# A bilinear interaction kernel: x turned by half as many transposes with straight and crosswise copies, and w cut at the edges of steps

## The chip, the cores and the metric

The kernel runs on one core of a Trainium2 chip. The metric is the device time of one execution in microseconds (us). Before the change it is 1345.8 us, the median of three runs (1344.6 to 1345.83). The profiled execution spans 1343.8 us.

## The reference

The input x holds 4096 samples (B) of 32 fields (F), each a vector of 64 numbers (D), in float32. For each of the 496 pairs of fields i < j there is a 64x64 matrix W. The output is, for every sample and pair, the vector x_i times W, multiplied elementwise by x_j:

```python
idx_i, idx_j = np.triu_indices(F, k=1)      # 496 pairs, ordered by i, then j
vi = inputs[:, idx_i, :]
vj = inputs[:, idx_j, :]
vidots = jnp.einsum('bpd,pde->bpe', vi, W)
return vidots * vj                          # 4096 x 496 x 64 float32
```

The output has 520 MB, x has 33.6 MB and W 8.1 MB. The profile counts 41.68 MB read from HBM and 520.09 MB written.

## The kernel before

The batch is taken in 16 blocks of 256 samples, each as NB = 2 tiles of 128 samples, so there are 32 tiles. `p0[i]` is the number of the first pair with left field i.

**Loads of w.** The 496 matrices are loaded as rows of 4096 numbers (16 KB), one pair to an SBUF partition, in four parts. Parts 0, 1 and 2 go out on SyncE's queue, between the loads of x, part 3 later on ScalarE's queue:

```python
cuts = [*range(0, NP, P), NP]               # 0, 128, 256, 384, 496
wrows = list(zip(cuts[:-1], cuts[1:]))
...
def load_w(c, eng=nc.sync):
    a, b = wrows[c]
    raw[c] = pool.tile([P, D * D], F32, tag=tag, name=f"raw_{c}")
    eng.dma_start(out=raw[c][: b - a, :], in_=wflat[a:b])
...
new_x(0)
load_x(0, nc.sync, 0, 1)                    # the first tile of block 0
load_w(0)
load_w(1)
load_x(0, nc.sync, 1, NB)
load_w(2)
new_x(1)
load_x(1, nc.sync)
```

Each part is then reordered (`order_w`, copies on VectorE, GpSimd or ScalarE), turned by TensorE (`turn_w`) and copied into `wT[c]`, where columns 0 to 31 of every W lie on partitions 0 to 63, one row of W to a partition, and columns 32 to 63 on partitions 64 to 127. Part 0 is done ahead of everything; the reorder copies and turns of parts 1 to 3 stand between the first steps:

```python
for c, orders, turns in (
    (1, (2, 4, 8, 10), (4, 7, 12, 15)),     # at these places of the schedule
    (2, (17, 22, 27, 32), (19, 24, 29, 34)),
    (3, (54, 54, 55, 55), (57, 60, 63, 66)),
):
```

**Turning x.** The matmul needs each field with D on the partitions. As the two halves of W's columns lie on different halves of the partitions, each field is needed on both halves. A transpose turns two neighbouring fields at once, and the kernel before takes overlapping pairs (s, s+1), (s+1, s+2), ..., so each field is turned twice: once into the lower, once into the upper half. A slot of zeros stands ahead of field 0.

```python
RUN = 2 * BANK // P                          # 8
def turn_x(blk, k, q, copy):
    pt = psum.tile([P, RUN, P], F32, tag="ps", name=...)
    for n in range(RUN):
        s = k * F + q * RUN + n
        nc.tensor.transpose(pt[:, n, :], xs[blk][:, s : s + 2, :].rearrange("p f d -> p (f d)"), ident)   # line 143
    xT = xtpool.tile([P, RUN, P], F32, tag="xT", name=...)
    copy(xT, pt)                             # line 147, on ScalarE
    return xT
...
AHEAD = 4                                    # a group is asked for so many steps early
at = place[t, first[q * RUN - 1] if q else 0] - AHEAD
```

**Steps.** A step takes up to CH = 16 pairs with the same left field. Two matmuls, one for each half of W's columns, fill two PSUM banks; a step that straddles two parts of w takes two for each part. VectorE multiplies by x_j into an output tile, or, for some steps (`aside`), ScalarE copies and GpSimd multiplies:

```python
for c, (lo, hi) in enumerate(wrows):
    lo, hi = max(pa, lo), min(pa + m, hi)
    if lo < hi:
        for h in range(2):
            n = i + 1 - h
            nc.tensor.matmul(                # line 244
                ps[:, h, lo - pa : hi - pa, :],
                xT[blk, kt, n // RUN][h * D : (h + 1) * D, n % RUN, :],
                wT[c][h * D : (h + 1) * D, lo - wrows[c][0] : hi - wrows[c][0], :],
                start=True, stop=True)
...
if i in aside and c0 == 0 and s not in no_aside:
    nc.scalar.copy(tmp, src)                 # line 258
    nc.gpsimd.tensor_mul(dst, tmp, xj)       # line 259
else:
    nc.vector.tensor_mul(dst, src, xj)       # line 261
```

**Outputs.** The pairs of a tile are cut into five groups of about 100 pairs. Each has an output tile (`ot`, three buffers, of which parts 0 and 1 of w use two at the start), and when its last step is done SyncE sends it to HBM in one transfer. The first three tiles are interleaved group by group, so that the later parts of w are needed later.

**Loads of x** after the first two blocks go out on ScalarE's queue in one transfer of 128 rows. For every third block the load is cut: 120 rows on GpSimd's queue in two transfers, and the other 8 rows in two transfers of 5 and 3 rows on ScalarE's queue (`load_fifteen`). `turn_engines` sends small transfers on GpSimd's queue.

Of the kernel before, what the change touches and what calls it, by code (L numbers as in the profile page):

```python
# [8 lines left out]
F32 = mybir.dt.float32  # L9
# [3 lines left out]
def kernel(  # L13
# [16 lines left out]
    nc = tc.nc  # L30

    B, F, D = x.shape
    P = 128
    NB = 2
    assert 2 * D == P and B % (NB * P) == 0
    NBLK = B // (NB * P)
    NP = F * (F - 1) // 2
    E2 = D // 2
    BANK = 512
    CH = BANK // E2  # L40
    RUN = 2 * BANK // P
    p0 = [i * (F - 1) - i * (i - 1) // 2 for i in range(F)]


# [3 lines left out]

    aside = (1, 3, 5, 7, 9, 11, 13)

    cuts = [*range(0, NP, P), NP]
    wrows = list(zip(cuts[:-1], cuts[1:]))

    const = ctx.enter_context(tc.tile_pool(name="const", bufs=1))
    xpool = ctx.enter_context(tc.tile_pool(name="xpool", bufs=2))
    xtpool = ctx.enter_context(tc.tile_pool(name="xtpool", bufs=4))
    tpool = ctx.enter_context(tc.tile_pool(name="tpool", bufs=4))
    opool = ctx.enter_context(tc.tile_pool(name="opool", bufs=3))
    psum = ctx.enter_context(tc.tile_pool(name="psum", bufs=4, space=bass.MemoryType.PSUM))

    ident = const.tile([P, P], F32, tag="ident", name="ident")
    make_identity(nc, ident)

    xs = {}

    def rows_of(dram: bass.AP, blk: int) -> bass.AP:
        return dram[blk * NB * P : (blk + 1) * NB * P]

    def new_x(blk: int):

        xs[blk] = xpool.tile([P, 1 + NB * F, D], F32, tag="xs", name=f"xs_{blk}")
        nc.gpsimd.memset(xs[blk][:, 0, :], 0.0)  # L72

    def load_x(blk: int, eng, k0: int = 0, k1: int = NB):
        src = rows_of(x, blk).rearrange("(p k) f d -> p (k f) d", k=NB)
        eng.dma_start(out=xs[blk][:, 1 + k0 * F : 1 + k1 * F, :], in_=src[:, k0 * F : k1 * F, :])

# [6 lines left out]
    def turn_engines(k: int):  # L86
        n = k if k > 1 else 17
        c = used[0] % 8
        used[0] += 1
        src = x[: NB * n].rearrange("(p k) f d -> p k f d", k=NB)  # L90
        tc.keep_in_program_order(
            nc.gpsimd.dma_start(out=scratch[:n, :, c : c + 1], in_=src[:, :, 0, 0:1])  # L92
        )

    def load_fifteen(blk: int):
        rows = rows_of(x, blk).rearrange("(p k) f d -> p k f d", k=NB)
        dst = xs[blk][:, 1:, :].rearrange("p (k f) d -> p k f d", k=NB)
        for a, b in ((SWR, SWR + 5), (SWR + 5, P)):
            nc.scalar.dma_start(out=xs[blk][a:b, 1:, :], in_=rows[a:b].rearrange("p k f d -> p (k f) d"))
        for h in range(2):  # L100
            cut = slice(h * F // 2, (h + 1) * F // 2)
            tc.keep_in_program_order(
                nc.gpsimd.dma_start(out=dst[:SWR, :, cut, :], in_=rows[:SWR, :, cut, :])  # L103
            )
            turn_engines(1)
# [7 lines left out]
    def load_w(c: int, eng=nc.sync):  # L113

        a, b = wrows[c]
        pool, tag = ((opool, "ot"), (opool, "ot"), (const, "w3"), (const, "w3"))[c]
        raw[c] = pool.tile([P, D * D], F32, tag=tag, name=f"raw_{c}")
        eng.dma_start(out=raw[c][: b - a, :], in_=wflat[a:b])

    def order_w(c: int, k: int, copy):  # L120
        r = wrows[c][1] - wrows[c][0]
        rp = tpool.tile([P, EU, 2, D], F32, tag="tmp", name=f"rp_{c}_{k}")
        src = raw[c][:r, :].rearrange("p (d h e) -> p e h d", h=2, d=D)
        copy(rp[:r], src[:, k * EU : (k + 1) * EU])  # L124
        return rp

    def turn_w(c: int, k: int, rp, copy):
        r = wrows[c][1] - wrows[c][0]
        if c not in wT:
            wT[c] = const.tile([P, r, E2], F32, tag=f"w{c}", name=f"wT_{c}")  # L130
        pt = psum.tile([P, EU, P], F32, tag="ps", name=f"ptw_{c}_{k}")
        for n in range(EU):
            nc.tensor.transpose(  # L133
                pt[:, n, :r], rp[:r, n].rearrange("p h d -> p (h d)"), ident[:r, :r]
            )
        copy(wT[c][:, :, k * EU : (k + 1) * EU], pt[:, :, :r].rearrange("p e r -> p r e"))  # L136

    def turn_x(blk: int, k: int, q: int, copy):

        pt = psum.tile([P, RUN, P], F32, tag="ps", name=f"ptx_{blk}_{k}_{q}")  # L140
        for n in range(RUN):
            s = k * F + q * RUN + n
            nc.tensor.transpose(  # L143
                pt[:, n, :], xs[blk][:, s : s + 2, :].rearrange("p f d -> p (f d)"), ident
            )
        xT = xtpool.tile([P, RUN, P], F32, tag="xT", name=f"xT_{blk}_{k}_{q}")
        copy(xT, pt)  # L147
        return xT


# [8 lines left out]
    first = {}  # L159
# [11 lines left out]
    place = {ts: n for n, ts in enumerate(sched)}  # L171


    AHEAD = 4
    due: dict = {}
    for t in range(NT):
        for q in range(F // RUN):
            at = place[t, first[q * RUN - 1] if q else 0] - AHEAD
            due.setdefault(max(0, at), []).append(("x", t // NB, t % NB, q))
    for c, orders, turns in (  # L180
        (1, (2, 4, 8, 10), (4, 7, 12, 15)),
# [9 lines left out]
    loads[place[LEAD, LATE]] = 2  # L191

    new_x(0)
    load_x(0, nc.sync, 0, 1)
# [6 lines that stand above are left out]
    turn_engines(5)  # L201

    v, p, a = nc.vector.tensor_copy, nc.gpsimd.tensor_copy, nc.scalar.copy
    xT, rps = {}, {}
    xT[0, 0, 0] = turn_x(0, 0, 0, a)
    due[0] = [d for d in due[0] if d != ("x", 0, 0, 0)]
    for k, copy in enumerate((v, v, v, a)):
# [5 lines left out]
    for s, (t, st) in enumerate(sched):  # L213
        blk, kt = divmod(t, NB)
        g, i, c0, m = steps[st]
        if s in loads:
            new_x(loads[s])
            if loads[s] % 3 == 1:
                load_fifteen(loads[s])
            else:  # L220
                load_x(loads[s], nc.scalar)
        for what, *args in due.get(s, ()):
            if what == "x":
                xT[tuple(args)] = turn_x(*args, a)
            elif what == "turn":
                turn_w(*args, rps.pop(tuple(args)), a)
            else:
                c, k = args
                rps[c, k] = order_w(c, k, (v, v, p, v)[c] if k % 2 == 0 else (v, v, p, a)[c])
                if (c, k) == (2, NU - 1):  # L230
                    load_w(3, nc.scalar)

        base, end = groups[g]
        pa = p0[i] + c0
        if pa == base:
            ots[t] = opool.tile([P, cap, D], F32, tag="ot", name=f"ot_{t}_{g}")
        ot = ots[t]
        ps = psum.tile([P, 2, CH, E2], F32, tag="ps", name=f"ps_{s}")
        for c, (lo, hi) in enumerate(wrows):
            lo, hi = max(pa, lo), min(pa + m, hi)  # L240
            if lo < hi:
                for h in range(2):
                    n = i + 1 - h
                    nc.tensor.matmul(  # L244
                        ps[:, h, lo - pa : hi - pa, :],
                        xT[blk, kt, n // RUN][h * D : (h + 1) * D, n % RUN, :],
                        wT[c][h * D : (h + 1) * D, lo - wrows[c][0] : hi - wrows[c][0], :],
                        start=True,
                        stop=True,
                    )  # L250
        o = pa - base
        j = 1 + kt * F + i + 1 + c0
        dst = ot[:, o : o + m, :].rearrange("p m (h e) -> p m h e", h=2)
        src = ps[:, :, :m, :].rearrange("p h m e -> p m h e")
        xj = xs[blk][:, j : j + m, :].rearrange("p m (h e) -> p m h e", h=2)
        if i in aside and c0 == 0 and s not in no_aside:
            tmp = tpool.tile([P, CH, 2, E2], F32, tag="tmp", name=f"tmp_{s}")
            nc.scalar.copy(tmp, src)  # L258
            nc.gpsimd.tensor_mul(dst, tmp, xj)  # L259
        else:  # L260
            nc.vector.tensor_mul(dst, src, xj)  # L261

        ends = (p0[2], end) if s < NS and (t, g) == (0, 0) else (end,)
        if pa + m in ends:
            n0 = p0[2] if len(ends) > 1 and pa + m == end else base
            nc.sync.dma_start(
                out=rows_of(out, blk).rearrange("(p k) n d -> p k n d", k=NB)[:, kt, n0 : pa + m, :],
                in_=ot[:, n0 - base : pa + m - base, :],
            )
# [28 lines left out]
```

## Time and profile before

| | before |
|---|---|
| time, median of 3 | 1345.8 us |
| span of the profiled execution | 1343.8 us |
| mean granted TensorE clock | 0.959 |
| transposes of x on PE (line 143) | 1024, 142.0 us busy |
| matmuls on PE (line 244) | 6272 records, 1017.8 us busy |
| copies of turned x on ScalarE (line 147) | 128 of 1012 ns, 129.5 us |
| multiplications on VectorE (line 261) | 1252, 944.8 us |
| output transfers | 161, 2880 to 3360 KB most of them, 16.3 to 17.1 us from issue to landing |
| mean DMA rate | 419 GB/s |

The span is the time from the first to the last instruction on the core. An engine's busy share is an average over the whole span. TensorE is shown as PE (matmuls and transposes) and PEld (loads of the stationary operand), VectorE as DVE, ScalarE as ACT, GpSimd as POOL and SyncE as SP. The row DMA gives the mean busy share of the core's 16 DMA engines, and GB/s what they moved. In a list of waits each line names who waited for whom, the sum in us, the number of times and the longest. In a line of the timeline, brackets hold the idle time ahead of it and what ended it; `x3` is a count of instructions merged into the line.

### The profile page before, as it was taken

The page shows a single profiled execution, that of the slowest core. Times are in us where ns is not written, and L with a number is a line of the kernel's source. Part 1 is how long each engine was busy: PE and PEld are TensorE (multiplying, and loading weights), DVE is VectorE, ACT ScalarE, POOL GpSimd, SP SyncE. Part 2 cuts the span into 40 slices and gives each one's busy share as a digit, 9 for nine tenths or more (in the row PEclk, how much of TensorE's full clock was granted, in tenths as well). Part 3 has the DMA queues.
Part 4 walks back from the last instruction along what each step waited for, and adds up shares of the span by engine and source line. Part 5 has one row for each costly group of instructions (what it writes and reads, how often), then busy time and mean ns, then how long its engine had stood idle before and what let it go on. Part 6 is the DMA issues. An engine that isn't in the chain of part 4 may idle for free.

```text
span 1343.8 us, 17902 instructions
## 1 busy us (share of the span) xinstructions
PE 1163.9 (87%) x7424; PEld 680.1 (51%) x7424; DVE 956.0 (71%) x1262; ACT 374.1 (28%) x367; POOL 544.7 (41%) x264
## 2 busy tenths in 40 slices
PE   6989889888898888888889888888988889989894
PEld 4555545545455454455445554444554545545552
DVE  5778767766677677776758777576876767767774
ACT  3432222223232232222232222232222323223321
POOL 1813424444243445333444434442444424344431
PEclk9989999999999899998989999899899989989997
DMA  9999999999999999999999999999999999999997
GB/s 394 371 427 410 427 422 433 429 421 430 422 430 426 431 427 407 427 424 429 432 420 424 404 424 431 425 430 416 419 421 411 428 425 427 423 423 431 423 415 320
DMA packets 28258, 562.95 MB, mean 419 GB/s; under 512 B 3456, under 2 KB 3456, under 8 KB 5504
## 3 DMA queue, kind: packets, MB, share of 16 engines
q1 hardware_dynamic: 24048, 530.59, 93.0%
q10 hardware_dynamic: 1632, 23.33, 4.2%
q0 software_dynamic: 2496, 7.88, 1.5%
q8 instruction: 58, 0.95, 0.3%
q14 instruction: 24, 0.20, 0.0%
HBM read 41.68 MB, written 520.09 MB: 418 GB/s over the span
## 4 chain that ended last, share of the span: by engine, by line
DMA 50%; PE 23%; DVE 16%; POOL 6%; issue 3%; ACT 1%; DVEq 0%; SPq 0%; POOLq 0%; ACTq 0%
DMA out_dram<-ot 50%; PE ps L244 18%; DVE ot L261 16%; POOL ot L259 5%; PE ptx L143 4%; PE ptw L133 1%; DMA raw<-in_L_rec_W_dram 1%; POOL scratch L92 1%; ACT tmp L258 1%; POOL xs L103 0%; DVE rp L124 0%; POOL rp L124 0%; DVEq L261 0%; ACT wT L136 0%; POOL xs L72 0%
## 5 line engine op out<-in xcount | busy, mean ns | idle before, releaser
L261 DVE TENSOR_TENSOR ot<-ps,xs 128x1024 f32<-128x1024 f32 (+15 forms) x1252 | 944.8, 810 | 356.8 <-DMA out_dram<-ot 193.8
L244 PE MATMUL ps<-wT,xT 64*128 64x512 f32 (+13 forms) x6272 | 1017.8, 467 | 122.4 <-DVE ot L261 110.7
L244 PEld LDWEIGHTS ps<-wT,xT 64*128 64x128 f32 x6272 | 552.7, 193 | 553.1 <-DVE ot L261 289.0
L259 POOL TENSOR_TENSOR ot<-tmp,xs 128x1024 f32<-128x1024 f32 x220 | 519.0, 2360 | 622.1 <-ACT tmp L258 438.7
L258 ACT COPY tmp<-ps 128x1024 f32<-128x1024 f32 x220 | 222.7, 1012 | 468.3 <-PE ps L244 401.2
L147 ACT COPY xT<-ptx 128x1024 f32<-128x1024 f32 x128 | 129.5, 1012 | 451.1 <-PE ptx L143 451.1
L143 PE MATMUL ptx<-ident,xs 128*128 128x128 f32 x1024 | 142.0, 283 | 35.9 <-DVE ot L261 27.5
L143 PEld LDWEIGHTS ptx<-ident,xs 128*128 128x128 f32 x1024 | 111.8, 143 | 82.5 <-issue 41.9
L72 POOL MEMSET xs<- 128x64 f32 x16 | 2.4, 151 | 148.5 <-DVE ot L261 148.5
L133 PE MATMUL ptw<-ident,rp 128*128 128x128 f32 (+1 forms) x128 | 18.6, 298 | 3.9 <-DVE rp L124 3.9
L133 PEld LDWEIGHTS ptw<-ident,rp 128*128 128x128 f32 (+1 forms) x128 | 15.6, 156 | 10.3 <-DVE rp L124 5.0
L136 ACT COPY wT<-ptw 128x1024 f32<-128x1024 f32 (+1 forms) x15 | 14.8, 984 | 20.9 <-PE ptw L133 20.9
L124 DVE COPY rp<-raw 128x1024 f32<-128x1024 f32 (+1 forms) x9 | 10.7, 1221 | 10.8 <-DMA raw<-in_L_rec_W_dram 10.8
L92 POOL DMA_DIRECT2D scratch<-in_r_inputs_dram x10 | 9.1, 908 | 0.2 <-issue 0.2
L124 POOL COPY rp<-raw 128x1024 f32<-128x1024 f32 x4 | 7.9, 1979 | 0.1
L124 ACT COPY rp<-raw 112x1024 f32<-112x1024 f32 (+1 forms) x3 | 5.9, 1958 | 5.0 <-POOL ot L259 3.2
L103 POOL DMA_DIRECT2D xs<-in_r_inputs_dram x8 | 6.0, 753 | 1.4 <-issue 1.4
L136 DVE COPY wT<-ptw 128x1024 f32<-128x1024 f32 x1 | 1.2, 1224 | 2.9 <-PE ptw L133 2.9
L147 ACT ACT_TABLE_LOAD x1 | 1.3, 1283 | 0.7 <-PEq L285 0.7
masks.py:197 POOL MEMSET ident<- 128x128 f32 x1 | 0.2, 204 | 0.3 <-POOLq L285 0.3
masks.py:199 POOL TENSOR_SCALAR_AFFINE_SELECT ident<-ident 128x128 f32<-128x128 f32 x1 | 0.3, 288 | 0.0
L285 POOL MEMSET const-float32-0.0<- 128x1 f32 x1 | 0.1, 93 | 0.3 <-issue 0.3
(3 smaller groups left out, 0.3 us busy)
## 6 DMA issues: line engine op xcount, KB each, us to landing
out_dram<-ot SPq DMA_DIRECT2D x64, 3360.0 KB, 16.3
out_dram<-ot SPq DMA_DIRECT2D x32, 3168.0 KB, 16.4
out_dram<-ot SPq DMA_DIRECT2D x32, 3104.0 KB, 17.0
out_dram<-ot SPq DMA_DIRECT2D x31, 2880.0 KB, 17.1
xs<-in_r_inputs_dram ACTq DMA_DIRECT2D x10, 2048.0 KB, 17.3
xs<-in_r_inputs_dram POOLq DMA_DIRECT2D x8, 960.0 KB, 31.5
raw<-in_L_rec_W_dram SPq DMA_DIRECT2D x3, 2048.0 KB, 17.1
xs<-in_r_inputs_dram SPq DMA_DIRECT2D x2, 1024.0 KB, 5.2
```

The costliest lines, as they stand in the source:

```text
L72: nc.gpsimd.memset(xs[blk][:, 0, :], 0.0)
L92: nc.gpsimd.dma_start(out=scratch[:n, :, c : c + 1], in_=src[:, :, 0, 0:1])
L103: nc.gpsimd.dma_start(out=dst[:SWR, :, cut, :], in_=rows[:SWR, :, cut, :])
L124: copy(rp[:r], src[:, k * EU : (k + 1) * EU])
L133: nc.tensor.transpose(pt[:, n, :r], rp[:r, n].rearrange("p h d -> p (h d)"), ident[:r, :r])
L136: copy(wT[c][:, :, k * EU : (k + 1) * EU], pt[:, :, :r].rearrange("p e r -> p r e"))
L143: nc.tensor.transpose(pt[:, n, :], xs[blk][:, s : s + 2, :].rearrange("p f d -> p (f d)"), ident)
L147: copy(xT, pt)
L244: nc.tensor.matmul(ps[:, h, lo - pa : hi - pa, :], xT[blk, kt, n // RUN][h * D : (h + 1) * D, n % RUN, :], wT[c][h * D : (h + 1) * D, lo - ...
L258: nc.scalar.copy(tmp, src)
L259: nc.gpsimd.tensor_mul(dst, tmp, xj)
L261: nc.vector.tensor_mul(dst, src, xj)
```

## The change

The change has two parts.

**x.** Each field is turned once, in pairs that don't overlap: four transposes for eight fields, 16 for a tile of 32 fields in place of 32. Three ScalarE copies then write the result twice: straight (`xT[:, 0]`), and crosswise (`xT[:, 1]`), the lower half of the partitions to the upper half and the upper to the lower, so that every field is again on both halves. The slot of zeros goes, with its memset. A group of turned fields is asked for six steps ahead of the first step that uses it.

**w.** The parts end at pairs 118 = p0[4], 243 = p0[9], 371 = p0[15] + 11 and 496, so that two of the three inner cuts fall on edges of steps. The parts have 118, 125, 128 and 125 rows in place of 128, 128, 128 and 112. How a part is loaded (`load_w`) stays as it is.

The purpose is to take work from TensorE: fewer transposes, and fewer steps that need two matmuls a half.

```diff
--- before.py
+++ after.py
@@ -38,7 +38,7 @@
     E2 = D // 2
     BANK = 512
     CH = BANK // E2
-    RUN = 2 * BANK // P
+    RUN = 8
     p0 = [i * (F - 1) - i * (i - 1) // 2 for i in range(F)]
 
 
@@ -48,7 +48,7 @@
 
     aside = (1, 3, 5, 7, 9, 11, 13)
 
-    cuts = [*range(0, NP, P), NP]
+    cuts = [0, p0[4], p0[9], p0[15] + 11, NP]
     wrows = list(zip(cuts[:-1], cuts[1:]))
 
     const = ctx.enter_context(tc.tile_pool(name="const", bufs=1))
@@ -68,12 +68,11 @@
 
     def new_x(blk: int):
 
-        xs[blk] = xpool.tile([P, 1 + NB * F, D], F32, tag="xs", name=f"xs_{blk}")
-        nc.gpsimd.memset(xs[blk][:, 0, :], 0.0)
+        xs[blk] = xpool.tile([P, NB * F, D], F32, tag="xs", name=f"xs_{blk}")
 
     def load_x(blk: int, eng, k0: int = 0, k1: int = NB):
         src = rows_of(x, blk).rearrange("(p k) f d -> p (k f) d", k=NB)
-        eng.dma_start(out=xs[blk][:, 1 + k0 * F : 1 + k1 * F, :], in_=src[:, k0 * F : k1 * F, :])
+        eng.dma_start(out=xs[blk][:, k0 * F : k1 * F, :], in_=src[:, k0 * F : k1 * F, :])
 
 
 
@@ -94,9 +93,9 @@
 
     def load_fifteen(blk: int):
         rows = rows_of(x, blk).rearrange("(p k) f d -> p k f d", k=NB)
-        dst = xs[blk][:, 1:, :].rearrange("p (k f) d -> p k f d", k=NB)
+        dst = xs[blk].rearrange("p (k f) d -> p k f d", k=NB)
         for a, b in ((SWR, SWR + 5), (SWR + 5, P)):
-            nc.scalar.dma_start(out=xs[blk][a:b, 1:, :], in_=rows[a:b].rearrange("p k f d -> p (k f) d"))
+            nc.scalar.dma_start(out=xs[blk][a:b], in_=rows[a:b].rearrange("p k f d -> p (k f) d"))
         for h in range(2):
             cut = slice(h * F // 2, (h + 1) * F // 2)
             tc.keep_in_program_order(
@@ -137,14 +136,17 @@
 
     def turn_x(blk: int, k: int, q: int, copy):
 
-        pt = psum.tile([P, RUN, P], F32, tag="ps", name=f"ptx_{blk}_{k}_{q}")
-        for n in range(RUN):
-            s = k * F + q * RUN + n
+
+        pt = psum.tile([P, RUN // 2, P], F32, tag="ps", name=f"ptx_{blk}_{k}_{q}")
+        for u in range(RUN // 2):
+            s = k * F + q * RUN + 2 * u
             nc.tensor.transpose(
-                pt[:, n, :], xs[blk][:, s : s + 2, :].rearrange("p f d -> p (f d)"), ident
-            )
-        xT = xtpool.tile([P, RUN, P], F32, tag="xT", name=f"xT_{blk}_{k}_{q}")
-        copy(xT, pt)
+                pt[:, u, :], xs[blk][:, s : s + 2, :].rearrange("p f d -> p (f d)"), ident
+            )
+        xT = xtpool.tile([P, 2, RUN // 2, P], F32, tag="xT", name=f"xT_{blk}_{k}_{q}")
+        copy(xT[:, 0], pt)
+        copy(xT[D:, 1], pt[:D])
+        copy(xT[:D, 1], pt[D:])
         return xT
 
 
@@ -171,11 +173,11 @@
     place = {ts: n for n, ts in enumerate(sched)}
 
 
-    AHEAD = 4
+    AHEAD = 6
     due: dict = {}
     for t in range(NT):
         for q in range(F // RUN):
-            at = place[t, first[q * RUN - 1] if q else 0] - AHEAD
+            at = place[t, first[q * RUN]] - AHEAD
             due.setdefault(max(0, at), []).append(("x", t // NB, t % NB, q))
     for c, orders, turns in (
         (1, (2, 4, 8, 10), (4, 7, 12, 15)),
@@ -240,16 +242,15 @@
             lo, hi = max(pa, lo), min(pa + m, hi)
             if lo < hi:
                 for h in range(2):
-                    n = i + 1 - h
                     nc.tensor.matmul(
                         ps[:, h, lo - pa : hi - pa, :],
-                        xT[blk, kt, n // RUN][h * D : (h + 1) * D, n % RUN, :],
+                        xT[blk, kt, i // RUN][h * D : (h + 1) * D, (i + h) % 2, i % RUN // 2, :],
                         wT[c][h * D : (h + 1) * D, lo - wrows[c][0] : hi - wrows[c][0], :],
                         start=True,
                         stop=True,
                     )
         o = pa - base
-        j = 1 + kt * F + i + 1 + c0
+        j = kt * F + i + 1 + c0
         dst = ot[:, o : o + m, :].rearrange("p m (h e) -> p m h e", h=2)
         src = ps[:, :, :m, :].rearrange("p h m e -> p m h e")
         xj = xs[blk][:, j : j + m, :].rearrange("p m (h e) -> p m h e", h=2)
```

## The prediction

> **What bounds the kernel now.** I read the engine table and the 40 slices first, then the DMA queues, then the table by stage, then the start of the timeline. The engine table and the slices of the page:
>
> ```profile
> PE 1163.9 (87%) x7424; PEld 680.1 (51%) x7424; DVE 956.0 (71%) x1262; ACT 374.1 (28%) x367; POOL 544.7 (41%) x264
> DMA  9999999999999999999999999999999999999997
> q1 hardware_dynamic: 24048, 530.59, 93.0%
> q10 hardware_dynamic: 1632, 23.33, 4.2%
> q0 software_dynamic: 2496, 7.88, 1.5%
> q8 instruction: 58, 0.95, 0.3%
> ```
>
> No compute engine is full, but the DMA row shows 9 in every slice but the last, and the four queues together hold 93.0 + 4.2 + 1.5 + 0.3 = 99.0% of the 16 engines' span. On q1, 530.59 MB in 0.93 x 16 x 1343.8 us = 19,996 engine-microseconds is 26.5 GB/s for one engine. The table by stage (columns: stretch, its length, busy time of PE, PEld, DVE, ACT and POOL, granted clock, DMA share, GB/s) says where there is any slack:
>
> ```profile
> 0.00:15.00 15.00, 5.02 (x23) 4.66 (x24) 2.96 (x3) 5.28 (x4) 1.55 (x9) 1.00 0.88 358
> 30.00:60.00 30.00, 30.00 (x183) 17.25 (x182) 22.09 (x23) 14.18 (x14) 24.07 (x11) 1.00 0.93 379
> 90.00:150.00 60.00, 59.13 (x418) 36.27 (x418) 51.23 (x77) 15.59 (x16) 14.32 (x7) 1.00 0.98 412
> 150.00:400.00 250.00, 219.84 (x1398) 127.74 (x1397) 179.44 (x239) 69.12 (x69) 105.42 (x50) 0.96 1.01 428
> 400.00:1320.00 920.00, 803.91 (x5134) 465.83 (x5134) 660.81 (x877) 251.08 (x249) 387.42 (x182) 0.97 1.00 423
> ```
>
> Only before 150 us is PE full (30.00 of 30, 59.13 of 60) while the DMA falls short of its 428 GB/s. From 150 us on, the DMA share is 1.00 and compute waits for output buffers: in the waits, VectorE's wait for an output transfer is the largest of its own, and PE's weight loads wait for VectorE in turn.
>
> ```profile
> DVE ot L261 <- DMA out_dram<-ot: 193.8, 96, 5.9
> ```
>
> So the steady part is bound by the transfers, and what a change does there to PE is worth little. What it does to the transfers, or to their split over the 16 engines, counts in full.
>
> [...] Queue q10 carried 10 loads of x with 128 rows, 4 with 5 rows, 4 with 3 rows, and w's last part with 112 rows: 1280 + 20 + 12 + 112 = 1424 rows of 16,384 bytes, which is the 23.33 MB shown. Of 1632 packets 208 are left, and 11 x 16 + 4 x 5 + 4 x 3 = 208: the small loads post 5 and 3 completions, not 16. It does not settle the point I lean on, that 118 rows use 2 engines and 125 use 5, for "all rows, at most 16" would count the same here.
>
> [...] copies of 1024 and 896 columns take 1012 and 905 ns, so 0.836 ns a column and 156 ns fixed.
>
> **Part 1: the transposes and copies of x.** There are 32 tiles (16 blocks of 2).
> - PE: the page has 1024 transposes in 142.0 us, 0.139 us each. 512 go: −71 us of PE.
> - ScalarE: 128 copies of 1024 columns (129.5 us) become 384 of 512. By the slope above one takes 156 + 512 x 0.836 = 584 ns, if partitions crosswise cost nothing extra; 384 x 0.584 = 224 us, so +95 us, and ScalarE goes from 374 to about 469 us, some 35% of the span.
> - Latency of a group of eight fields: 8 x 0.139 + 1.01 = 2.1 us becomes 4 x 0.139 + 3 x 0.584 = 2.3 us. It is asked for 6 steps ahead and not 4, so this hides.
> - The one-slot memset (16 x 0.15 us on GpSimd) goes as well: nothing.
>
> **Part 2: w's parts end at step edges.** Steps that straddle two parts go from 3 a tile to 1 (only pair 371 lies inside a step). A straddled step costs 2 more matmuls in code, which are 4 more records (6272 records in 32 tiles are 196 a tile, twice the 98 in code). So 2 x 4 x 32 = 256 records go. Their fixed cost: 32 columns take 23.0 us / 256 = 0.090 us, 512 columns 492.6 / 1792 = 0.275 us, so 0.078 us at no columns; 256 x 0.078 = −20 us of PE. PE in all: 1164 − 71 − 20 = about 1073 us, 8% less. Beside a DMA share of 1.00 that is hidden. I allow −2 us for it.
>
> **Part 3: what the new cuts do to the loads of w.** This is the part I believe in. The parts have 118, 125, 128 and 125 rows of 16 KB in place of 128, 128, 128 and 112. [...]
> - part 0: 128/16 = 8 rows an engine before; 118 = 2 x 59 gives 2 engines with 59 rows each;
> - part 1: 8 before; 125 gives 5 engines with 25 rows each;
> - part 2: 8 and 8;
> - part 3: 112/16 = 7 before; 25 now.
>
> Engines 0 and 1 take part in all of them: 31 rows become 117, +86 rows. The time of a row is in the timeline of before (columns: start, length, engine, line, operation):
>
> ```profile
> 6.07 1.94 PE L143 MATMUL ptx<-ident,xs 128*128 128x128 f32 x8 [6.07 <-DMA xs<-in_r_inputs_dram]
> 10.83 2.96 DVE L124 COPY rp<-raw 128x1024 f32<-128x1024 f32 x3 [10.83 <-DMA raw<-in_L_rec_W_dram]
> 21.97 2.02 DVE L124 COPY rp<-raw 128x1024 f32<-128x1024 f32 x2
> 26.25 1.76 SPq L266 DMA_DIRECT2D out_dram<-ot  x2
> ```
>
> The first half tile of x is there at 6.07 us and part 0 of w, next in the queue, at 10.83 us: 4.76 us for 8 rows, 0.595 us a row (27.5 GB/s an engine). So engines 0 and 1 get 86 x 0.595 = **51 us** more to do, and they carry an equal eighth of every output with the rest, from a base that is already 99% busy.
>
> The same from the side of compute: part 0 lands at 6.07 + 59 x 0.595 = 41.2 us, not 10.8. Part 1 queues behind it on engines 0 and 1 and lands at 41.2 + 25 x 0.595 = 56.1 us. VectorE reorders part 1 as early as the third step, at 21.97 us before, so it stands still until 56: a delay of 34 us of everything that follows. Meanwhile engines 0 and 1 still have x and part 2 to fetch (2.4 + 4.8 + 4.8 us), to about 68 us, while the first outputs, issued at 26.25 before, now come at about 60: those two engines are never idle, and the other fourteen wait for them, because a buffer comes free only when all its shares have landed. Part 3 adds 18 rows, 11 us, which are in the 51.
>
> Sum. +51 us of engine time. The slack before 150 us fills partly: against 428 GB/s, 30 us at 379 lose 3.4 us, 60:90 (414 by the same table) 1.0, 60 us at 412 lose 2.2, together 6.6; I take −6. The wait for part 3, which shares its engines with outputs, can leave a bubble while VectorE and ScalarE reorder it: 0 to 8 us, I take +2. PE: −2. So 1345.8 + 51 − 6 + 2 − 2 = 1396.8. The view by compute gives less: 34 plus a stall of 8 to 18 us at part 3, less up to 9 us of PE saved in the three tiles of the start, so 33 to 43 us. Between the two, leaning to the engines, I choose **1391 us**, +3.4%.
>
> **Rivals.**
> - *The loads of w split evenly enough* (16 engines, or the rows cut otherwise). Then only PE gets lighter under a full DMA. For it: before does not show a case where "divides" and "at most 16" differ. Against it: [...] that the kernel before cuts an 8-row remnant into 5 and 3, and takes 120 rows on another queue, as one does who reckons with divisors. It gives 1335 to 1347 us.
> - *PE is the real limit.* For it: the chain that ended last has PE with 23%. Halving the transposes' 3.8% of it is 1.9% of 1344, 25 us; with most of the split matmuls 40 us, so 1305 to 1320. Against it: the chain has the output transfer with 50%, and the steady DMA share is 1.00. A gain of 2% would need the transfers themselves to be faster.
> - *ScalarE becomes the bound*, by longer holds of PSUM slots. At 35% busy with 6 steps of lead I see no more than a few us, 1345 to 1355.
> - *The backlog is worse*: other loads of x that also use the low engines, or a bubble at each buffer handed back late, 1400 to 1415.
>
> **Range and chances.** The main case (some 85%) has a spread of 15 us either way, from slack absorbed and the part 3 stall. The low end is pushed down a little for the mixed cases: 1370 to 1407. Below 1372.7 us (+2%) lie the first rival and the mildest form of the main case: slower by over 2% 0.85, within 2% 0.12, faster by over 2% 0.03.
>
> **What would show it.** Right: VectorE's first copy of w waits for about 41 us; the stretch 0 to 60 us moves few GB/s; PE about 1073 us with 512 transposes, ScalarE about 469 us; from 200 us on, the same pace as before. The queue counts tell the rule apart: q1 has 13 rows less and, with 2 and 5 completions in place of 16 and 16, 25 completions less, so 24010 packets (24035 if w still runs on 16 engines); q10 has 13 rows more and 11 completions less, 1634 (or 1645). Wrong: the first copy of w still at about 11 us, or a steady stretch that moves clearly more than 428 GB/s.

## The result and the profile after

The changed kernel takes 1413.55 us (median of 5 runs, 1412.89 to 1414.55) against 1345.8 us before: a ratio of 1.0506, with a 95% interval of 1.049 to 1.0521. It is slower by 68 us. The prediction was 1391 us with a range of 1370 to 1407 us: the sign and the main cause were right, the size was too small.

The page of the changed kernel, the engine table, the slices and the queues:

```profile
PE 1138.9 (81%) x6656; PEld 601.9 (43%) x6656; DVE 950.6 (67%) x1262; ACT 467.6 (33%) x623; POOL 542.6 (38%) x248
DMA  6268699999999999999999999999999999999997
q1 hardware_dynamic: 24010, 530.38, 89.2%
q10 hardware_dynamic: 1634, 23.54, 4.0%
```

The first five slices of the DMA row are no longer full; from the sixth on, the row is as before. The packet counts are the ones that the prediction gave for 2 and 5 engines, 24010 and 1634, to the packet. The DMA share says the same: 0.31 from 5 to 11 us is 5 of 16 engines, and 0.12 from 45 to 65 us is 2. So the 118 rows went out on 2 engines and the 125 rows on 5.

By stage (stretch, length, PE, PEld, DVE, ACT, POOL, clock, DMA share, GB/s):

```profile
0.00:15.00 15.00, 1.09 (x4) 0.71 (x4) 0.00 (x0) 3.03 (x4) 1.38 (x7) 1.00 0.57 184
30.00:60.00 30.00, 5.63 (x32) 5.42 (x32) 3.98 (x4) 4.06 (x4) 0.00 (x0) 1.00 0.38 119
60.00:90.00 30.00, 18.99 (x90) 9.70 (x92) 15.61 (x16) 9.24 (x12) 6.84 (x3) 0.77 0.32 133
90.00:150.00 60.00, 38.82 (x214) 20.41 (x210) 28.39 (x32) 21.71 (x23) 29.70 (x14) 0.84 0.82 345
400.00:1320.00 920.00, 789.88 (x4606) 414.95 (x4608) 660.17 (x883) 315.52 (x428) 378.18 (x169) 0.95 1.00 425
```

In the first 60 us PE does almost nothing, where before it was full from 30 to 60 us. From 400 us on the transfers move 425 GB/s, against 423 before. So the loss lies in the start; the dates of the outputs below place it before 156 us. The timeline shows which waits it consists of (start, length, engine, line, operation; in brackets the idle time and what ended it):

```profile
53.04 2.98 DVE L123 COPY rp<-raw 118x1024 f32<-118x1024 f32 x3 [53.04 <-DMA raw<-in_L_rec_W_dram]
68.07 1.03 DVE L123 COPY rp<-raw 125x1024 f32<-125x1024 f32 x1 [7.93 <-DMA raw<-in_L_rec_W_dram]
70.59 1.09 PE L143 MATMUL ptx<-ident,xs 128*128 128x128 f32 x4 [10.82 <-DMA xs<-in_r_inputs_dram]
146.83 3.83 ACT L123 COPY rp<-raw 125x1024 f32<-125x1024 f32 x2 [21.91 <-DMA raw<-in_L_rec_W_dram]
147.26 1.03 DVE L123 COPY rp<-raw 125x1024 f32<-125x1024 f32 x1 [17.10 <-DMA raw<-in_L_rec_W_dram]
```

In the list of waits (who for whom, sum, times, longest) the waits for w stand beside the one for output buffers, which was 193.8 us before:

```profile
DVE ot L262 <- DMA out_dram<-ot: 218.5, 98, 5.9
DVE rp L123 <- DMA raw<-in_L_rec_W_dram: 78.1, 3, 53.0
PE ptx L143 <- DMA xs<-in_r_inputs_dram: 17.3, 3, 10.8
```

Part 0 of w is there at 53.04 us (10.83 before), part 1 at 68.07, the second half of x's first block at 70.59, and part 3, issued at 109.25 us, at 146.83.

The output transfers date the loss. They are issued in the same order in both kernels, so the issue time of the n-th, taken from each trace, can be compared:

| output | before, us | after, us | later by, us |
|---|---|---|---|
| 1st | 26.25 | 80.68 | 54.4 |
| 8th | 70.52 | 123.59 | 53.1 |
| 9th | 84.60 | 155.49 | 70.9 |
| 31st | 264.3 | 334.2 | 69.9 |
| 81st | 674.1 | 742.7 | 68.6 |
| last | 1326.5 | 1393.8 | 67.3 |

So there are two steps, 54 us before the first output and 18 us between the 8th and the 9th, and then a slow recovery of 3.6 us.

### The profile page after: what moved, and what is told of

It is laid out like the page before. It is cut to its first block, busy times and chain, and to the rows that moved or that the text cites. A ratio compares the mean times of both kernels' runs of the same rounds, so it can differ in the third digit from the quotient of the medians.

```text
span 1411.1 us, 16692 instructions
## 1 busy us (share of the span) xinstructions
PE 1138.9 (81%) x6656; PEld 601.9 (43%) x6656; DVE 950.6 (67%) x1262; ACT 467.6 (33%) x623; POOL 542.6 (38%) x248
## 3 DMA queue, kind: packets, MB, share of 16 engines
q1 hardware_dynamic: 24010, 530.38, 89.2%
q10 hardware_dynamic: 1634, 23.54, 4.0%
## 4 chain that ended last, share of the span: by engine, by line
DMA 56%; PE 19%; DVE 13%; another core or an unknown queue 4%; POOL 3%; issue 2%; ACT 1%; DVEq 0%; SPq 0%; POOLq 0%; ACTq 0%
DMA out_dram<-ot 53%; PE ps L245 17%; DVE ot L262 13%; POOL ot L260 3%; DMA raw<-in_L_rec_W_dram 3%; PE ptx L143 1%; PE ptw L132 1%; ACT tmp L259 1%; POOL rp L123 0%; DVE rp L123 0%; DVEq L262 0%; ACT xT L149 0%; ACT xT L147 0%; ACT xT L148 0%
## 5 line engine op out<-in xcount | busy, mean ns | idle before, releaser
L245 PE MATMUL ps<-wT,xT 64*128 64x512 f32 (+12 forms) x6016 | 1047.4, 488 | 163.4 <-DVE ot L262 158.7
L245 PEld LDWEIGHTS ps<-wT,xT 64*128 64x128 f32 x6016 | 531.8, 195 | 619.8 <-DVE ot L262 370.6
L147 ACT COPY xT<-ptx 128x512 f32<-128x512 f32 x128 | 74.9, 585 | 336.5 <-PE ptx L143 336.5
L143 PE MATMUL ptx<-ident,xs 128*128 128x128 f32 x512 | 85.3, 290 | 44.0 <-DVE ot L262 24.5
L143 PEld LDWEIGHTS ptx<-ident,xs 128*128 128x128 f32 x512 | 54.6, 142 | 117.5 <-DVE ot L262 85.9
L149 ACT COPY xT<-ptx 64x512 f32<-64x512 f32 x128 | 74.5, 582 | 1.5
L148 ACT COPY xT<-ptx 64x512 f32<-64x512 f32 x128 | 73.9, 577 | 1.5
L123 DVE COPY rp<-raw 125x1024 f32<-125x1024 f32 (+1 forms) x9 | 9.1, 1047 | 78.1 <-DMA raw<-in_L_rec_W_dram 78.1
L132 PE MATMUL ptw<-ident,rp 125*128 125x125 f32 (+2 forms) x128 | 18.6, 300 | 47.0 <-DVE rp L123 47.0
L132 PEld LDWEIGHTS ptw<-ident,rp 125*128 125x128 f32 (+2 forms) x128 | 15.6, 157 | 54.0 <-DVE rp L123 47.4
L135 ACT COPY wT<-ptw 128x1000 f32<-128x1000 f32 (+2 forms) x15 | 14.8, 988 | 17.9 <-PE ptw L132 14.9
```

The costliest lines, as they stand in the source:

```text
L132: nc.tensor.transpose(pt[:, n, :r], rp[:r, n].rearrange("p h d -> p (h d)"), ident[:r, :r])
L143: nc.tensor.transpose(pt[:, u, :], xs[blk][:, s : s + 2, :].rearrange("p f d -> p (f d)"), ident)
L147: copy(xT[:, 0], pt)
L148: copy(xT[D:, 1], pt[:D])
L149: copy(xT[:D, 1], pt[D:])
L245: nc.tensor.matmul(ps[:, h, lo - pa : hi - pa, :], xT[blk, kt, i // RUN][h * D : (h + 1) * D, (i + h) % 2, i % RUN // 2, :], wT[c][h * D : ...
```

## The experiments

The theory: the loads of 118 and 125 rows go out on 2 and 5 engines, and compute waits for them. The rivals: the new way of turning x (three copies, asked for earlier) costs the time; or PE was the bound all along. Times of the kernel before in these comparisons are 1345.85 to 1346.28 us.

### Each half of the change alone

The turning of x alone, with the old cuts:

```diff
-    cuts = [0, p0[4], p0[9], p0[15] + 11, NP]
+    cuts = [*range(0, NP, P), NP]
```

> The changed kernel with the cuts of w as before (128, 128, 128, 112), so the x part of the change alone. Theory: 1335 to 1348 us, at most 1% from the kernel before, because the transfers bind and PE's saving is hidden. Rival (x part costs): clearly over 1360 us. Rival (PE binds): under 1325 us.

Measured: 1345.16 us, ratio 0.9994 (0.9986 to 1.0003). The x half of the change is worth nothing that can be told from zero, in either direction. It does half the transposes and ScalarE works 467.7 us in place of 374.1, and both are hidden.

The new cuts alone, in the kernel before:

```diff
-    cuts = [*range(0, NP, P), NP]
+    cuts = [0, p0[4], p0[9], p0[15] + 11, NP]
```

> The kernel before with the new cuts of w alone. Theory: nearly the whole loss, 1400 to 1414 us, a little less than the changed kernel because the second tile's transposes stand behind the first two steps. Rival (x part costs most): under 1375 us.

Measured: 1414.48 us, ratio 1.051 (1.0495 to 1.0524). The cuts alone, with the loads that come with them, make the whole loss. I had thought it would be slightly less than in the changed kernel; it isn't.

### The cuts, or the shape of their loads?

First, every part loaded as a multiple of 16 rows and a remainder:

```diff
-        eng.dma_start(out=raw[c][: b - a, :], in_=wflat[a:b])
+        e = (b - a) // 16 * 16
+        eng.dma_start(out=raw[c][:e, :], in_=wflat[a : a + e])
+        if e < b - a:
+            eng.dma_start(out=raw[c][e : b - a, :], in_=wflat[a + e : b])
```

> The changed kernel, but each part of w is loaded in two transfers: first the largest multiple of 16 rows (112), then the remainder (6 or 13 rows). Theory (row counts of 118 and 125 run on 2 and 5 engines): the whole loss goes, first copy of w at about 11 us, 1335 to 1348 us. Rival (the new turning of x with its three copies, or asking for it earlier, costs the time): 1380 us or more remain.

Measured: 1353.69 us, ratio 1.0059 (1.0046 to 1.0071). Most of the loss is gone, but not the last 8 us: part 0 is there at 14.62 us, not at 11. The engines have nearly the same number of rows to fetch as before (32 on the fullest in place of 31), so something makes the rows themselves slower. The stretches of this kernel show it (same columns as above):

```profile
10.00:15.00 5.00, 0.00 (x0) 0.00 (x0) 0.39 (x1) 0.40 (x1) 0.00 (x0) 1.00 1.00 216
15.00:25.00 10.00, 5.99 (x32) 5.77 (x32) 3.73 (x4) 4.39 (x4) 0.00 (x0) 0.97 0.98 221
```

All 16 engines are busy (1.00, 0.98) and move 216 and 221 GB/s, half of what such a share moves elsewhere. So 112 rows and a remainder are not loaded as 128 rows are, though the 112 do use 16 engines: q1 counts 24054 packets, 44 more than in the changed kernel, which are 16 + 6 + 16 + 13 completions in place of 2 + 5. Which of the two transfers makes the difference was not tried.

Second, the new cuts kept, but each part loaded, reordered and turned with 128 rows, some of them a neighbour's (the line with `r` stands in both `order_w` and `turn_w`):

```diff
+    wload = [(min(a, NP - P), min(a, NP - P) + P) for a, _ in wrows]
...
-        a, b = wrows[c]
+        a, b = wload[c]
...
-        r = wrows[c][1] - wrows[c][0]
+        r = wload[c][1] - wload[c][0]
...
-                        wT[c][h * D : (h + 1) * D, lo - wrows[c][0] : hi - wrows[c][0], :],
+                        wT[c][h * D : (h + 1) * D, lo - wload[c][0] : hi - wload[c][0], :],
```

> The changed kernel with the new cuts, but every part is loaded, reordered and turned with 128 rows (parts 0, 1 and 3 with some rows of their neighbours, 16 rows more in all, 0.6 us of transfer), so that each load is of 128 rows and 128 partitions. Theory (what is lost comes from the shape of the loads alone, also the 8 us that 112 rows and a remainder still lost): 1343 to 1349 us. Rival (those 8 us belong to the new cuts or to the turning of x): 1352 to 1356 us.

Measured: 1344.73 us, ratio 0.999 (0.9984 to 0.9997). The whole loss is gone with the whole change in place, and part 0 is there at 10.59 us:

```profile
10.59 2.96 DVE L124 COPY rp<-raw 128x1024 f32<-128x1024 f32 x3 [10.59 <-DMA raw<-in_L_rec_W_dram]
```

So neither the cuts nor the turning of x costs anything; the shape of the loads does. This version is also what the change is worth when its loads are mended: about 1 us, 0.1%.

### The two delays apart

Parts 0 and 1 alone loaded evenly (`e = (b - a) // 16 * 16 if c < 2 else b - a`, otherwise as in the first edit of the section above):

> The changed kernel with parts 0 and 1 of w loaded as a multiple of 16 rows plus remainder; part 3 stays one transfer of 125 rows. In the changed kernel's trace the outputs are 54 us late after the start and 70 us late after part 3. Theory (two separate delays that add up): about 1413.5 - 54 = 1360 us. Rival (an engine's sum of rows counts, each row 0.6 us; part 3 is 18 rows too many): 1357 us or less. Rival (all loss is at the start): about 1345 us.

Part 3 alone loaded evenly (`if c == 3`):

> The changed kernel with part 3 alone loaded evenly; parts 0 and 1 as changed. Theory (two delays that add up): about 1413.5 - 17 = 1397 us. Rival (backlog of the busiest engines decides, 11 us for part 3): 1402 us.

Measured: 1369.4 us (ratio 1.0174, 1.0157 to 1.0191) and 1396.89 us (1.0378, 1.0362 to 1.0393). Part 3 is worth 1413.55 − 1396.89 = 16.7 us from the one side and 1369.4 − 1353.69 = 15.7 us from the other; parts 0 and 1 are worth 44.2 us and 43.2 us, and the 8 us that the even loads still lost are left. The delays add up. The first of the two came out at 1369 and not at 1360 as I had thought, because I had taken the whole 54 us off and not reckoned with the 8 us left. A bound by each engine's own sum of rows (1357 us or less) doesn't fit.

Part 3 in the changed kernel shares its five engines with output transfers:

```profile
112.00:132.00 20.00, 14.82 (x86) 7.79 (x82) 10.12 (x12) 7.59 (x11) 11.24 (x5) 0.96 1.00 419
135.00:147.00 12.00, 0.00 (x0) 0.00 (x0) 0.00 (x0) 0.17 (x1) 0.00 (x0) 0.50 0.32 137
147.00:155.00 8.00, 5.08 (x23) 3.29 (x24) 7.05 (x9) 5.30 (x5) 0.00 (x0) 0.55 0.15 63
```

From 112 to 132 us the rate is full. Then a share of 0.32 is 5.1 of 16 engines: part 3 and the rest of the outputs on its engines, while no compute engine has work. When part 3 has landed at 146.83 us, it still takes until 155.49 for the next output, and the DMA share in that time is only 0.15.

### Does the second tile's turn hold up the start?

```diff
             at = place[t, first[q * RUN]] - AHEAD
+            if t == 1 and q == 0:
+                at += 2
```

> The changed kernel, but the second tile's first transposes stand behind the first two steps, as in the kernel before, and not ahead of them. In the changed kernel's trace PE stands before them until 70.6 us, when the second half of x's first block lands. Theory: these two steps' work (about 3 us) moves ahead of the wait, 1409 to 1412 us. Rival (this wait is what added 8 us to the start): 1404 to 1407 us.

Measured: 1414.17 us, ratio 1.0508 (1.0494 to 1.0523). Neither is right: nothing is gained. The first output goes out at 77.0 us in place of 80.7, but the third at 90.6 in place of 89.4. Which of the first steps stands behind PE's wait made no difference to the end here.

### Why a row took 0.80 us and not 0.60

Part 0 took 53.04 − 6.06 = 47 us for 59 rows, 0.80 us a row. The loads of few engines put last in the queue, behind the loads of x and part 2:

```diff
     load_x(0, nc.sync, 0, 1)
-    load_w(0)
-    load_w(1)
     load_x(0, nc.sync, 1, NB)
     load_w(2)
     new_x(1)
     load_x(1, nc.sync)
+    load_w(0)
+    load_w(1)
```

> The changed kernel with another order of the first loads: the first tile of x, its second half, part 2 of w and the next block first, and only then parts 0 and 1 of w, so that their few engines work alone. In the changed kernel's trace a row of part 0 took 0.80 us on average, 0.61 while few engines ran and 1.2 while all did. Theory (the other loads slow the rows down): 0.61 us a row, part 0 after 18 + 36 = 54 us, part 1 about 15 us later, and no wait for x any more, so 1400 to 1408 us. Rival (a transfer on 2 engines is slow by itself): part 0 after 18 + 47 = 65 us and 1420 us or more.

Measured: 1410.12 us, ratio 1.0475 (1.046 to 1.0491), a little over the theory's 1400 to 1408, and under the rival's 1420. Part 0 is there at 53.98 us, 36 us after the other loads end at about 18 us: 0.61 us a row. Alone, the few engines run at full rate each:

```profile
20.00:54.00 34.00, 0.00 (x0) 0.00 (x0) 0.02 (x1) 0.02 (x1) 0.00 (x0) 1.00 0.19 82
```

82 GB/s over 0.19 x 16 = 3.0 engines (a mean: from 30 to 60 us the share was 0.14, a little over two) is 27 GB/s each, where the prediction had 27.5 for an engine in the kernel before. So the rows of a transfer on 2 engines are not slow by themselves; they are slow beside other loads, 0.80 us and not 0.61. The gain for the end is small all the same, since it starts so much later.

Part 0 alone with 118 rows, the others cut into 112 and a remainder (`if c > 0`):

> The changed kernel with only part 0 of w loaded as one transfer (118 rows, 2 engines); parts 1 and 3 evenly. Theory: part 0 lands at 41 us if the slow rows came from part 1's five engines, at 45 to 53 us if any loads beside it slow it; then about 35 to 40 us of delay, 1380 to 1388 us, and no stall at part 3.

One run: 1393.9 us, and part 0 at 58.50 us. Both were expected lower: beside the loads of 112 rows and a remainder a row of part 0 took 0.89 us.

Part 0 alone with 118 rows, the others with 128 (the 128-row version, with `wload[0] = wrows[0]` and the load cut to its rows):

> As the version with 128 rows in every load, but part 0 is loaded with 118 rows (2 engines). With parts 1 and 3 cut into 112 and 13 rows, part 0 landed at 58.5 us, 0.89 us a row. Theory (transfers over partitions in another way than usual slow the loads beside them, and here two engines alone do so): 43 to 50 us. Rival (any load beside it slows it, the loads of x and w together): 53 us or more. Rival (only few engines, no slowing): 41.5 us.

One run: 1391.55 us, and part 0 at 55.67 us. The theory's 43 to 50 us was too little; the figure is that of the rival, by which any load beside it slows it, those of 128 rows too. The slowing goes both ways: a load on two engines was enough to slow everything beside it, all engines together to 218 GB/s at a share of 0.99.

```profile
10.00:15.00 5.00, 0.00 (x0) 0.00 (x0) 0.00 (x0) 0.00 (x0) 0.00 (x0) 1.00 1.10 239
15.00:25.00 10.00, 0.00 (x0) 0.00 (x0) 0.00 (x0) 0.00 (x0) 0.00 (x0) 1.00 0.99 218
```

The version with 128 rows in every load, which differs from this one in part 0's load alone, moved twice as much from 15 to 25 us, and so did the kernel before; one line of each, in this order:

```profile
15.00:25.00 10.00, 9.34 (x52) 6.43 (x52) 6.62 (x6) 5.70 (x7) 1.62 (x1) 1.00 1.02 435
15.00:25.00 10.00, 8.90 (x55) 5.80 (x55) 7.39 (x7) 4.64 (x5) 1.19 (x1) 1.00 1.03 437
```

What is unusual in those loads, if it isn't the number of engines? My guess was: which partitions a transfer writes together. Four versions of the kernel before load parts 0 to 2 in two transfers each, with all 16 engines busy (a share of 1.01 to 1.02 in the stretches below); part 3 is loaded as before. Halves of rows: 64 rows into partitions 0 to 63, then 64 into 64 to 127.

```diff
-        eng.dma_start(out=raw[c][: b - a, :], in_=wflat[a:b])
+        for e in (0, P // 2):                       # parts 0 to 2
+            eng.dma_start(out=raw[c][e : e + P // 2, :], in_=wflat[a + e : a + e + P // 2])
```

> The kernel before, with parts 0 to 2 of w each loaded as two transfers of 64 rows: partitions 0 to 63, then 64 to 127. Both use all 16 engines with 4 rows each, 8 rows an engine as before; [...] Theory (a load that does not go over all 128 partitions in the usual way [...] runs at half rate): part 0 there at about 15.6 us in place of 10.8, part 1 at about 25, the time 1352 to 1362 us. Rival (only the number of rows an engine counts): 10.8 us and 1345 to 1347 us.

Halves of columns: 128 partitions twice, 8 KB each.

```diff
+        for e in (0, D * D // 2):                   # parts 0 to 2
+            eng.dma_start(out=raw[c][:, e : e + D * D // 2], in_=wflat[a:b, e : e + D * D // 2])
```

> Control: the kernel before, with parts 0 to 2 of w each loaded as two transfers of 128 rows, first the left 8 KB of each row, then the right. As many transfers as with halves of rows, but each over all 128 partitions. Both theories: part 0 there at about 11 us, 1345 to 1348 us. If two transfers in place of one are what costs: as slow as with halves of rows.

These two differ in the rows read together and in the partitions written together. Two more change one side each. Reading as in the first, writing as in the second:

```diff
+        for e in (0, 1):                            # parts 0 to 2; half = D * D // 2
+            src = wflat[a + e * P // 2 : a + (e + 1) * P // 2].rearrange("r (h n) -> (r h) n", h=2)
+            eng.dma_start(out=raw[c][:, e * half : (e + 1) * half], in_=src)
```

> The kernel before; parts 0 to 2 of w loaded in two transfers each, each of which reads 64 whole rows (as with halves of rows) but spreads them over all 128 partitions, half a row to each. The weights land in another order than the matmuls take them for, so the output is not the reference's; the work and its timing are the same. If which partitions of SBUF are written together is what halved the rate: full rate, part 0 there at about 11 us, 1345 to 1348 us. If which rows of HBM are read together is what did it: part 0 at about 16.5 us and about 1362 us.

And reading as in the second, writing as in the first:

```diff
+        for e in (0, 1):                            # parts 0 to 2; half = D * D // 2
+            src = wflat[a:b, e * half : (e + 1) * half].rearrange("(r h) n -> r h n", h=2)
+            dst = raw[c][e * P // 2 : (e + 1) * P // 2, :].rearrange("r (h n) -> r h n", h=2)
+            eng.dma_start(out=dst, in_=src)
```

> The counterpart: each of the two transfers reads half of each of 128 rows (as with halves of columns, which ran at full rate) but writes 64 partitions, two half rows to each. Again the weights land in another order, so the output is not the reference's. If the partitions written together are what counts: half rate, part 0 at about 16.5 us, about 1362 us. If the rows read together are: about 11 us and 1345 to 1348 us.

| each transfer reads | writes | part 0 there, us | time, us | ratio (95% interval) |
|---|---|---|---|---|
| 64 whole rows | 64 partitions | 16.54 | 1362.8 | 1.0128 (1.0114 to 1.0142) |
| half of 128 rows | 128 partitions | 11.26 | 1345.3 | 0.9997 (0.9989 to 1.0006) |
| 64 whole rows | 128 partitions | 11.21 | 1345.99 | 0.9998 (0.9989 to 1.0007) |
| half of 128 rows | 64 partitions | 18.41 | 1363.56 | 1.0126 (1.0109 to 1.0143) |

The stretch from 10 to 15 us, in the order of the table, one fence for each kernel:

```profile
10.00:15.00 5.00, 0.00 (x0) 0.00 (x0) 0.00 (x0) 0.00 (x0) 0.00 (x0) 1.00 1.01 213
```

```profile
10.00:15.00 5.00, 2.66 (x13) 2.66 (x14) 2.96 (x3) 2.61 (x2) 0.00 (x0) 1.00 1.02 429
```

```profile
10.00:15.00 5.00, 2.71 (x13) 2.71 (x14) 2.96 (x3) 2.67 (x2) 0.00 (x0) 1.00 1.02 431
```

```profile
10.00:15.00 5.00, 0.43 (x3) 0.03 (x1) 0.00 (x0) 1.01 (x1) 0.00 (x0) 1.00 1.01 210
```

The DMA share is the same in all four, 1.01 to 1.02; 64 partitions move 210 to 213 GB/s, 128 partitions 429 to 431. The reading side plays no part here. Nor does the number of transfers, two a part in all four, nor the size of the pieces: the last three all move 8 KB at a time, and only the last of them is slow. So, with all 16 engines busy too, a busy share of 1.00 is no sign of full rate. Why 64 partitions take half the rate was not shown. That one load on two engines with 59 rows each halves the rate of all sixteen is measured above (218 GB/s against 435); by what means it does so was not shown either.

## Why the prediction was wrong in size

The mechanism was right in that a few engines, 2 and 5 of 16, carry the loads of w and compute waits for them, until 53.04 and 68.07 us. The terms that failed are the time of a row while other loads run (0.80 us and not 0.595), the moment from which the delay counts (17.79 us and not 21.97), the slack, and the cost of part 3 (17.8 us and not 13).

**Bound and steady part: right.** The transfers stay the bound after the start (a share of 1.00 and 425 GB/s from 400 to 1320 us); of the lateness of the outputs 3.6 us are made up between the 9th and the last, where I had −2.

**Two and five engines: right.** That 118 and 125 rows go out on 2 and 5 engines was my assumption, which the counts of before did not settle; the packet counts of the changed kernel are those computed from it, 24010 and 1634. That parts 0 and 1 share engines shows in the landings (that they are numbers 0 and 1 no trace shows): part 1 lands 68.07 − 53.04 = 15.0 us behind part 0, where 25 x 0.595 = 14.9 was computed.

**The time of a row: wrong, and the largest single error.** "4.76 us for 8 rows, 0.595 us a row" came from loads over 128 partitions, and I multiplied it by 59. In the changed kernel a row of part 0 took 0.80 us, since other loads ran beside it at half rate: part 0 at 53.04 us and not 41.2, +11.9 us.

**The moment before: misread.** "VectorE reorders part 1 as early as the third step, at 21.97 us before" took the second of these copies. The first stood at 17.79 us in the same timeline of before:

```profile
17.79 1.02 DVE L124 COPY rp<-raw 128x1024 f32<-128x1024 f32 x1
21.97 2.02 DVE L124 COPY rp<-raw 128x1024 f32<-128x1024 f32 x2
```

That is +4.2 us. With both corrections the delay is 68.07 − 17.79 = 50.3 us in place of 34; the outputs came 54.4 us later. The other 4 us fit what PE does next: it waits 2.5 us more, for the second half of x's first block, and then 16 matmul records take 5.58 us where 8 took 1.93 us before, at a granted clock (the share of TensorE's full clock) of 0.61 from 70.6 to 77.2 us, and of 1.00 from 18 to 27 us before. Together that is an estimate of 2.5 + 5.58 − 2 x 1.93 = 4.2 us, from these traces. The version with the later turn of x took 3.7 us off the first output and nothing off the end, so what these 4 us are worth by themselves stays open.

**The sum: wrong.** 1345.8 + 51 − 6 + 2 − 2 is 1390.8, not 1396.8: the 6 us of slack were named but not taken off in the total. So 1391 was not a middle between two views, as the text says, but the sum of the engines itself; the view by compute gave 1379 to 1389.

**The slack that fills: wrong.** I reckoned with 6 us of slack, since engines 0 and 1 "are never idle". Two engines were indeed busy up to about 80 us (a share of 0.12 from 45 to 65 us, 0.11 from 76 to 80), but compute came just as late as they did, and between the first output and the eighth only 54.4 − 53.1 = 1.3 us were made up.

**Part 3: mis-sized.** In the engine's sum it had 11 us of rows and 2 of bubble. It cost 17.8 us between the 8th and the 9th output (16.7 us in the experiment). The view by compute had 8 to 18 for it and was the better one: what counts is how long VectorE and ScalarE wait and how long the refill takes, not the rows alone. I had leaned to the engines, whose sum (1357 us or less with parts 0 and 1 loaded evenly) the run at 1369.4 us does not fit.

**Parts 1 and 2 of the prediction: ScalarE right, PE wrong.** ScalarE: 469 predicted, 467.6 measured; crosswise copies take 577 and 582 ns, straight ones 585, where 584 was computed. PE: about 1073 predicted, 1138.9 measured. The 512 transposes took 85.3 us, 0.167 each and not 0.139, and the 6016 matmul records 1047.4 us, more than the 6272 before. Busy time on PE grew elsewhere, at a granted clock of 0.944 in place of 0.959; what else is in it was not tried. It costs nothing, as the x half alone shows with PE at 1138.5 us and no change in time.

**The rivals.** None of the first three happened. The fourth, "the backlog is worse", named the measured time (1400 to 1415), but partly by luck: there is a bubble at part 3, while more comes from the slowed rows, which it didn't have. The sum of 67 us is 54.4 − 1.3 + 17.8 − 3.6.

## What to carry to other kernels

A load's row count was part of its speed here: part 0 was there at 10.59 us with 128 rows and at 53.04 us with 118. When a load stands at the start, where everything waits for it, try it over all 128 partitions, even if that means some rows of a neighbour: here this brought 1413.55 us down to 1344.73. Before taking a time from one shape to another, ask which partitions are written together (128 went at 429 to 431 GB/s, 64 at 210 to 213), and what else loads at that time (a row of part 0 took 0.61 us once the loads on all 16 engines had ended and 0.80 beside them); read GB/s beside the DMA share, as a share of 1.00 went with 216 GB/s in one stretch here and with 425 in another. And with transfers as the bound, lighter compute was worth nothing here: half the transposes brought 0.1% at best.

## What had not been expected of the hardware

In the stretches shown from the start, all 16 engines together ran at half rate (210 to 239 GB/s at a share of about 1.0) with loads over 64 partitions, with loads of 112 rows and a remainder, and with one load on 2 engines beside loads of 128 rows. Beside output transfers, which read SBUF, part 3's five engines did not do this: 419 GB/s from 112 to 132 us.

SyncE's queue itself also stood still. Two issues of the changed kernel, of loads of x that follow the few-engine loads in the queue (start, length), and the same issues in the kernel before:

```profile
1.94 9.11 SPq L75 DMA_DIRECT2D xs<-in_r_inputs_dram  x1
11.56 20.93 SPq L75 DMA_DIRECT2D xs<-in_r_inputs_dram  x1
```

```profile
2.13 0.67 SPq L76 DMA_DIRECT2D xs<-in_r_inputs_dram  x1
3.53 0.49 SPq L76 DMA_DIRECT2D xs<-in_r_inputs_dram  x1
```

They took 9.11 and 20.93 us in place of 0.67 and 0.49. For part of that time only about five of the 16 engines had anything to move (shares of 0.31 and 0.32):

```profile
5.00:11.00 6.00, 1.09 (x4) 0.71 (x4) 0.00 (x0) 1.74 (x3) 0.00 (x0) 1.00 0.31 131
27.00:32.00 5.00, 0.00 (x0) 0.00 (x0) 0.00 (x0) 0.00 (x0) 0.00 (x0) 1.00 0.32 133
```

From 13 to 27 us, between these two stretches, all were busy, at half rate (218 GB/s at a share of 0.98). What the standing queue costs by itself was not tried.
